# LoRA activations of a gated FFN: the 128x128 transpose moves from TensorE to DVE blocks and two DRAM transfers, and the LoRA steps are issued apart

## The chip, the cores and the metric

The kernel runs on one core of a Trainium2 chip. Time is device time in microseconds; the median of three runs counts. Profiles come from one profiled execution, whose own time is given beside its span. PE is the matrix engine (TensorE), PEld its weight loads, DVE the vector engine, ACT the scalar engine, POOL the GpSimd engine, SP the engine that only issues transfers. L with a number is a line of the kernel.

## The reference

64 batches of 64 channels and 1024 features (4096 rows in all, called tokens) first have their channels mixed by one of 16 matrices, then pass a linear layer with a mixture of eight low-rank (LoRA) experts, of which a gate takes the best two. All is float32.

```python
def _L0_cond_ref(x, weights, condition):
    W = weights[condition]                        # (64, 64, 64)
    return jnp.einsum('bct,bcd->bdt', x, W)

def _L0_ffn_ref(x, gate_w, base_w, base_b, lora_A, lora_B):
    gate_logits = jnp.einsum('bsd,ed->bse', x, gate_w)          # e = 8
    weights, selected = jax.lax.top_k(gate_logits, K)           # K = 2
    weights = jax.nn.softmax(weights.astype(jnp.float32), axis=2)
    result = jnp.einsum('bsd,od->bso', x, base_w) + base_b
    w_full = jnp.sum(jax.nn.one_hot(selected, E) * weights[..., None], axis=2)
    low = jnp.einsum('bsd,erd->ebsr', x, lora_A)                # r = 16
    lora_out = jnp.einsum('ebsr,eor,bse->bso', low, lora_B, w_full)
    return result + SCALING * lora_out

x = x + _L0_ffn_ref(_L0_cond_ref(x, ...), ...)
```

## The kernel before

**Tiles.** The 4096 tokens are 32 tiles of 128. For each tile the kernel multiplies the transposed input (`xT`) with one wide matrix of 1160 columns: 128 of LoRA A (8 experts of rank 16), 8 of the gate, 1024 of the base. The columns are cut into chunks c = 0, 1, 2 of 384, 388 and 388; chunk 0 holds LoRA A, the gate and 248 base columns. This product is called z. Mixing the channels is a product from the left, so it is done on z afterwards, with a block-diagonal 128x128 matrix (`bd`, loaded by index by `load_cond`).

**Three matmuls for one.** float32 products are made of a high and a low part (`xh`, `xl`; `wh`, `wl`; `zh`, `zl`; `bdh`, `bdl`; `lth`, `ltl`; `lbh`, `lbl`): hi x hi, hi x lo, lo x hi. ACT makes the high part (`copy`, L232), DVE the low part (`sub`, L229).

**Stages of z.** The first four tiles are plain (`PLAIN`). The other 28 go in pairs, each pair's z by 20 block products p1 to p20 of sums of blocks instead of 24 (a fast matrix product). `Operands` loads blocks of x into 18 units of `xr` and makes their sums on DVE (L290), `split_x` splits them, `zstep` (L409) issues the matmuls, `keep`, `pass_on` (L710) and `mix` (L727) recombine the results from the PSUM banks z0 to z3. The order of products is the list `ORDER`: `HEAD`, then for each further pair a mix of the last five products of one pair (`TAIL`) and those of the next; for the last two pairs the list `FINAL` (t: the earlier pair, p: the later).

**After z.** `chunk` calls `post` for each tile i and chunk c:
- c = 0: `sums` (L441) mixes the channels into bank a0 or a1. `gate` copies the 136 columns of Low and logits to `low` (L472), finds the top two and their softmax weights (L478 to L484), and scales Low by them (L485). `tr` transposes the scaled Low (128 tokens x 128) on PE against the identity into the same bank (L492), and splits it into `lth` (ACT) and `ltl` (DVE). A second `sums` adds the LoRA part, `lth`/`ltl` times `lbh`/`lbl`, onto the 248 base columns.
- c = 1, 2: one step of six matmuls, LoRA and channel sums together, into bank o0 or o1; for the last two tiles two steps, LoRA first.
- `finish` (L451) adds the bank to `xtok`, where x plus bias lies (`load_tok`: SP loads x, POOL accumulates the bias, L376); `store` sends it out, by POOL (L458), for the last two tiles by SP (L461). There are three `xtok` buffers. The first four tiles have x and bias added by POOL afterwards (`late_sum`).

**Order.** Nothing is scheduled by hand beyond `ORDER`. Each step is told to the class `Program` with an engine, a cost, what it reads and writes and a due time (`pr.horizon`); `run` then lays the steps out in planned time, and issues on each engine in that order. A step with `first` goes ahead of others 1.2 us (`MARGIN`) after its inputs are ready by the plan; a transfer is planned at 2.0 us (`FLIGHT`) plus its bytes, and the order of the products on PE is kept by the name "order". On the chip each engine works through its instructions in the planned order, and waits where an input is late; SP and POOL wait likewise before they issue a transfer.

Of the kernel before, what the change touches and what calls it, by code (L numbers as in the profile page):

```python
# [24 lines left out]
ER = E * R  # L25
SCALING = 2.0
LOWEST = -3.0e38
NTOK = B * C
NT = NTOK // P
# [3 lines left out]
N0 = NG + T - 2 * W  # L33
# [3 lines left out]
NPAIR = NT // 2  # L37
NPLAIN = 2
TOP = 3.0e38
NWARM = 39  # L40

PE, ACT, DVE, POOL, SP = "PE", "ACT", "DVE", "POOL", "SP"
# [4 lines left out]
ISSUE = 0.45  # L47
# [4 lines left out]
AHEAD = 10.0  # L52
MARGIN = 1.2
COL, SET = 0.000418, 0.014
LEAST = 0.111
PAIR = 27.3
LAG, LAST = 16.0, 8.0
SOONER = 2.0
# [4 lines left out]
            p12="f9", p13="f13", p14="r", p15="f15", p16="a11", p17="a22", p18="f18", p19="f19", p20="f11")  # L63
BANK = dict(p6="R", p16="X", p7="Q", p5="X", p19="Y", p17="X", p11="R", p13="R", p18="X", p4="Q", p20="Q", p3="X",
            p1="R", p10="X", p12="X", p14="Y", p15="Y", p2="Y", p8="Y", p9="Y")
FIRST_ONLY = ("p4", "p10", "p12", "p20")
OPENS = ("p6", "p16", "p7", "p19")
HEAD = ("p6", "p16", "p7", "p5", "p19", "p17", "p11", "p13", "p18", "p4", "p20", "p3", "p1", "p10", "p12")
TAIL = ("p14", "p15", "p2", "p8", "p9")

FINAL = "t14 p6 t15 p16 p7 t2 p5 t8 p17 t9 p11 p4 p13 p19 p18 p20 p14 p3 p10 p15 p12 p1 p2 p8 p9".split()

SPLITS = (("f6", "a11"), ("s", "f5"), ("f19", "a22"), ("f11", "f13"), ("f18", "a24"), ("f3", "f1"), ("a13", "f9"),
          ("r", "f15"), ("f2", "f8"))
# [3 lines left out]
class Program:  # L78
# [7 lines left out]
    def add(self, engine, cost, fn, reads=(), writes=(), due=None, first=False, size=0.0, early=None, port=False,  # L86
            after=0.0):

        n = len(self.steps)
        engine, cost = (e if isinstance(e, (list, tuple)) else [e] for e in (engine, cost))
        deps = set()
        for b in list(reads) + list(writes):
            if b in self.writer:
                deps.add(self.writer[b])
        for b in writes:
            deps.update(self.readers.get(b, ()))
        for b in reads:
# [67 lines left out]
def cond_ffn_kernel(ctx, tc, xT, x, idx, cw, wall, bias, lb, out):  # L167
# [21 lines left out]
    nc = tc.nc  # L189
    eng = {ACT: nc.scalar, DVE: nc.vector, POOL: nc.gpsimd}  # L190
    sb = ctx.enter_context(tc.tile_pool(name="sb", bufs=1))
    ps = ctx.enter_context(tc.tile_pool(name="ps", bufs=1, space=bass.MemoryType.PSUM))

    def many(n, shape, dt, name):
        return [sb.tile(shape, dt, name=f"{name}{j}") for j in range(n)]
# [3 lines left out]
    ident = sb.tile([P, P], F32, name="ident")  # L199
# [7 lines left out]
    lth, ltl = many(2, [P, P], F32R, "lth"), many(2, [P, P], F32R, "ltl")  # L207
    ltr = ltl[1].bitcast(F32)
    scratch = {nm: many(2, [P, w], F32, nm) for nm, w in (
        ("mx", 8), ("l2", 14), ("e", E), ("wf", E), ("s", 1), ("nm", 1), ("r", 1))}  # L210
# [14 lines left out]
    pr = Program()  # L225
    add = pr.add

    def sub(e, o, a, b):
        eng[e].tensor_tensor(o, a, b.bitcast(F32), ALU.subtract)  # L229

    def copy(e, o, a):
        (nc.scalar.copy if e == ACT else nc.vector.tensor_copy)(o, a)  # L232
# [3 lines left out]
    def take(kind, n):  # L236
        turns[kind] = turns.get(kind, -1) + 1
        return turns[kind] % n
# [67 lines left out]
    raw, hi, lo = {}, {}, {}  # L306
# [92 lines left out]
    def mm_cost(n):  # L399
        return max(COL * n + SET, LEAST)  # L400

# [62 lines left out]
    def gate(i, b):  # L464

        v = {k: t[i % 2] for k, t in scratch.items()}
        t = low[i % 2]
        lg, lg14 = t[:, ER:NG], t[:, ER:]  # L470
        zc = [("low", i % 2)]
        add(ACT, 0.3, lambda e: copy(e, t[:, :NG], bank[b][:, :NG]), [b], zc)  # L472

        def op(o, a, f, eng=DVE, cost=0.17, port=False):
            add(eng, cost, lambda e: f(), [(b, i % 2) for b in a], [(b, i % 2) for b in o], port=port)

        stt = nc.vector.scalar_tensor_tensor
# [4 lines left out]
        op(["wf", "s"], ["l2", "e"], lambda: stt(v["wf"], v["l2"][:, :E], LOWEST, v["e"], ALU.is_equal, ALU.mult,  # L482
                                                 accum_out=v["s"]), cost=0.3, port=True)
        op(["r"], ["s"], lambda: nc.vector.reciprocal(v["r"], v["s"]))  # L484
        op(["low"], ["wf", "r"], lambda: stt(  # L485
            t[:, :ER].rearrange("p (e r) -> p e r", e=E), t[:, :ER].rearrange("p (e r) -> p e r", e=E), v["r"],
            v["wf"].unsqueeze(2).broadcast_to([P, E, R]), ALU.mult, ALU.mult), cost=0.3, port=True)

    def tr(i, b):

        h, l, tp = lth[i % 2], ltl[i % 2], bank[b][:, N0:N0 + P]
        add(PE, 0.107, lambda e: nc.tensor.matmul(tp, low[i % 2][:, :ER], ident, is_transpose=True, start=False,  # L492
                                                  stop=False, skip_group_check=True),
            [("low", i % 2), "ident"], [b], first=i < NT - 2)
        add(ACT, 0.25, lambda e: copy(e, h, tp), [b], [("lth", i % 2)])
        add(DVE, 0.25, lambda e: sub(e, l, tp, h), [b, ("lth", i % 2)], [("ltl", i % 2)])

    held = {}

    def post(i, c, q):  # L500

        if c == 0:
            b = held[i] = f"a{i % 2}"
            if i >= NT - 2:
                pr.horizon -= SOONER
# [4 lines left out]
            finish(i, c, b)  # L510
            if i >= NT - 2:
                pr.horizon += SOONER
            return
        else:
            b = f"o{take('o', 2)}"
            if i >= NT - 2:
                sums(i, c, b, with_lora=True, start=True)
                sums(i, c, b, q, (0, 1, 2), stop=True)
            else:
                sums(i, c, b, q, (0, 1, 2), True, True, True)  # L520
        finish(i, c, b)


# [6 lines left out]
    t = 4.9  # L530
# [4 lines left out]
        ends_plain = t  # L535
    ORDER = [(NPLAIN, p) for p in HEAD]
    for q in range(NPLAIN, NPAIR):
        if q == NPAIR - 2:
            ORDER += [(q + (p[0] == "p"), "p" + p[1:]) for p in FINAL]
            break  # L540
        nxt = HEAD
        mixed = ("p14", nxt[0:1], "p15", nxt[1:2], "p2", nxt[2:3], "p8", "p9", nxt[3:])
        for p in mixed:
            ORDER += [(q, p)] if isinstance(p, str) else [(q + 1, n) for n in p]
    ends = {}
    for q, p in ORDER:
        for f in range(2):
# [252 lines left out]
    for q, p in ORDER:  # L800
        pr.horizon = ends[q] + (LAST if q == NPAIR - 1 else LAG)
        if q not in pairs:
            pairs[q] = Pair(q)
        if (q, p) == (NPLAIN, HEAD[3]):
            load_pair(q)
        pairs[q].product(p)
        if p == TAIL[-1] and q < NPAIR - 1:

            load_pair(q + 1)
    pr.run()  # L810
# [39 lines left out]
```

## Time and profile before

| what | us |
|---|---|
| median of three runs | 460.18 (459.96 to 460.42) |
| the profiled execution | 460.46 |
| its span, first to last instruction | 458.7 |
| PE busy | 452.3 |
| DVE busy | 383.4 |
| DVE busy in 136 to 163 us, about one pair's turn | 22.84 of 27.00 |
| ACT busy in the same stretch | 13.05 |
| chain of waits: share of PE | 93% |

The mean granted clock of PE is 1.000. A stage's PE time is read from where its matmuls start, since each takes some 340 ns and the next starts about 178 ns later. The DMA line of the page gives the mean busy share of 16 DMA engines; "us to landing" is the time from a transfer's issue until its data are there.

### The profile page before, as it was taken

The numbers are of one execution on the slowest core, as the hardware profiler recorded it, in microseconds if no ns is written. First come the engines' busy times: TensorE is split into PE (matmuls) and PEld (weight loads), VectorE is DVE, ScalarE is ACT, GpSimd is POOL, SyncE is SP. The second block draws the span as 40 slices with busy tenths as digits, with TensorE's granted clock in tenths as the row PEclk, the third lists the DMA queues.
The fourth block names the chain that finished last, engine by engine and source line by source line (L and its number), as shares of the span: only waits on it lengthen the run. The fifth ranks groups of instructions, "written<-read, shape, count | busy, mean of one in ns | idle before, by whom it ended". The sixth has DMA issues, their size and how long they took to land.

```text
span 458.7 us, 7562 instructions
## 1 busy us (share of the span) xinstructions
PE 452.3 (99%) x2615; PEld 449.0 (98%) x2615; DVE 383.4 (84%) x940; ACT 227.5 (50%) x520; POOL 88.8 (19%) x107
## 2 busy tenths in 40 slices
PE   8999999999999999999999999999999999999995
PEld 8999999999999999999999999999999999999995
DVE  5999997878989788796997979789797988888674
ACT  5864656543636345373543646355354544546231
POOL 3010215121303021120303003030120403103000
PEclk9999999999999999999999999999999999999999
DMA  8942739976778462764846566573655746456142
GB/s 284 336 126 42 160 98 205 214 215 198 176 211 202 172 161 88 215 128 167 188 137 189 119 185 150 172 181 110 196 120 177 182 128 195 114 176 148 48 137 91
DMA packets 36085, 75.00 MB, mean 164 GB/s; under 512 B 4416, under 2 KB 22096, under 8 KB 36048
## 3 DMA queue, kind: packets, MB, share of 16 engines
q0 software_dynamic: 10560, 36.72, 33.7%
q1 hardware_dynamic: 25200, 37.41, 26.0%
q10 hardware_dynamic: 288, 0.40, 0.3%
q8 instruction: 20, 0.33, 0.3%
q14 instruction: 17, 0.14, 0.1%
HBM read 57.74 MB, written 16.78 MB: 162 GB/s over the span
## 4 chain that ended last, share of the span: by engine, by line
PE 93%; DMA 5%; DVE 1%; SPq 1%; ACT 0%; issue 0%; ACTq 0%
PE ps_z L409 71%; PE ps_o L441 15%; PE ps_a L441 6%; DMA xtok<-in_lb 2%; DMA w_b<-in_w 2%; DMA xr<-in_xT 1%; PE ps_a L492 1%; SPq L324 0%; SPq L274 0%; DVE xtok L451 0%; DVE wl_b_b L229 0%; ACT wh_b_b L232 0%; DVE st L727 0%; ACTq L232 0%
## 5 line engine op out<-in xcount | busy, mean ns | idle before, releaser
L229 DVE TENSOR_TENSOR xl<-xr,xh 128x512 fp32r<-128x512 f32 (+1 forms) x138 | 92.3, 672 | 20.6 <-ACT xh L232 20.3
L409 PE MATMUL ps_z<-wh_t_p,xh 128*128 128x388 f32 (+1 forms) x308 | 105.3, 342 | 0.1
L409 PE MATMUL ps_z<-wl_t_p,xh 128*128 128x388 f32 (+1 forms) x308 | 104.3, 339 | 0.0
L409 PE MATMUL ps_z<-wh_t_p,xl 128*128 128x388 f32 (+1 forms) x308 | 104.3, 339 | 0.0
L232 ACT CAST xh<-xr 128x512 fp32r<-128x512 f32 (+1 forms) x136 | 82.5, 610 | 37.4 <-PE ps_z L409 32.8
L727 DVE TENSOR_TENSOR st<-ps_z,st 128x388 f32<-128x388 f32 x126 | 70.3, 559 | 21.0 <-PE ps_z L409 19.9
L290 DVE TENSOR_TENSOR xr<-xr 128x256 f32<-128x256 f32 (+1 forms) x139 | 69.7, 528 | 3.1 <-DMA xr<-in_xT 2.7
L409 PE MATMUL ps_z<-wh_b_p,xh 128*128 128x388 f32 (+1 forms) x180 | 61.4, 341 | 0.0
L409 PE MATMUL ps_z<-wh_b_p,xl 128*128 128x388 f32 (+1 forms) x180 | 60.8, 338 | 0.0
L409 PE MATMUL ps_z<-wl_b_p,xh 128*128 128x388 f32 (+1 forms) x180 | 60.8, 338 | 0.0
L409 PEld LDWEIGHTS ps_z<-wh_t_p,xh 128*128 128x128 f32 x308 | 57.8, 188 | 1.2 <-DVE st L727 0.7
L409 PEld LDWEIGHTS ps_z<-wl_t_p,xh 128*128 128x128 f32 x308 | 57.9, 188 | 0.0
L409 PEld LDWEIGHTS ps_z<-wh_t_p,xl 128*128 128x128 f32 x308 | 57.8, 188 | 0.0
L458 POOL DMA_DIRECT2D out<-xtok x30 | 16.8, 560 | 193.5 <-DVE xtok L451 92.2
L232 ACT CAST zh<-st 128x388 fp32r<-128x388 f32 (+1 forms) x70 | 36.2, 517 | 24.2 <-DVE st L727 17.0
L376 POOL DMA_DIRECT2D xtok<-in_bias x28 | 27.4, 980 | 97.3 <-DMA xtok<-in_x 90.0
L389 POOL DMA_INDIRECT bdr<-in_cw,rows x32 | 36.1, 1129 | 28.0 <-DVE zl L229 16.6
L710 ACT ACTIVATE ps_z<-ps_z 128x388 f32<-128x388 f32 x42 | 20.1, 478 | 41.1 <-PE ps_z L409 39.0
L451 DVE TENSOR_TENSOR xtok<-ps_o,xtok 128x388 f32<-128x388 f32 x56 | 31.0, 559 | 11.0 <-PE ps_o L441 10.6
L229 DVE TENSOR_TENSOR zl<-st,zh 128x388 fp32r<-128x388 f32 (+1 forms) x70 | 38.9, 556 | 1.5 <-ACT zh L232 1.2
L409 PEld LDWEIGHTS ps_z<-wh_b_p,xh 128*128 128x128 f32 x180 | 33.8, 188 | 0.2
L409 PEld LDWEIGHTS ps_z<-wl_b_p,xh 128*128 128x128 f32 x180 | 33.8, 188 | 0.0
(130 smaller groups left out, 871.1 us busy)
## 6 DMA issues: line engine op xcount, KB each, us to landing
xr<-in_xT SPq DMA_DIRECT2D x128, 128.0 KB, 3.1
xtok<-in_bias POOLq DMA_DIRECT2D x32, 512.0 KB, 7.2
out<-xtok POOLq DMA_DIRECT2D x30, 512.0 KB, 3.1
xtok<-in_x SPq DMA_DIRECT2D x28, 512.0 KB, 3.7
w_b<-in_w SPq DMA_DIRECT2D x10, 388.0 KB, 5.8
xtok<-in_x POOLq DMA_DIRECT2D x4, 512.0 KB, 6.2
out<-xtok SPq DMA_DIRECT2D x4, 194.0 KB, 2.5
bdr<-in_cw,rows POOLq DMA_INDIRECT x32, 5.3
```

What stands on the lines that cost most here:

```text
L229: eng[e].tensor_tensor(o, a, b.bitcast(F32), ALU.subtract)
L232: (nc.scalar.copy if e == ACT else nc.vector.tensor_copy)(o, a)
L290: add(DVE, tt_cost(2 * P * len(os)), lambda e: nc.vector.tensor_tensor(some(xr, os), some(xr, xs), some(xr, ys), f), [("xr", u) for u in s ...
L376: add(POOL, 1.1, lambda e: nc.gpsimd.dma_start(xtok[j], bias.broadcast_to([P, T]), accum_op=ALU.add), writes=keys, size=TWICE * 4.0 * T * P)
L389: add(POOL, 1.04, lambda e: nc.gpsimd.indirect_dma_start(out=bdr[j], out_offset=None, in_=cw, in_offset=bass.IndirectOffsetOnAxis(ap=rows[ ...
L409: nc.tensor.matmul(z, l[:, j, n], w.ap()[:, f, :cols], start=(start and q == 0), stop=(stop and q == 2), skip_group_check=True)
L441: nc.tensor.matmul(d, l, r, start=(start and m == 0), stop=(stop and m == len(mms) - 1), skip_group_check=True)
L451: add(DVE, 0.09 + 0.00104 * (s.stop - s.start), lambda e: nc.vector.tensor_tensor(xtok[j][:, o], bank[b][:, s], xtok[j][:, o], ALU.add), [ ...
L458: add(POOL, 1.0, lambda e: nc.gpsimd.dma_start(out[i * P:(i + 1) * P, o], xtok[j][:, o]), src, size=4.0 * P * (o.stop - o.start))
L492: add(PE, 0.107, lambda e: nc.tensor.matmul(tp, low[i % 2][:, :ER], ident, is_transpose=True, start=False, stop=False, skip_group_check=True),
L710: add(ACT, 0.2 + 0.00085 * W, lambda e: nc.scalar.mul(z[b], z[x], scale), [BANKS[x]], [BANKS[b]])
L727: add(DVE, 0.09 + 0.00104 * W, lambda e: nc.vector.tensor_tensor(unit(u), a(), b(), f), reads, [ukey(u)])
```

## The change

- For tiles 0 to 27, `tr` no longer uses PE. DVE transposes the scaled `low` within blocks of 32x32 into a new SBUF tile `ltt`. SP writes that to a DRAM tile `there`, and SP reads it back, 128 bytes at a time, so that the blocks come to their transposed places. `lth` and `ltl` are then split from `ltt` in SBUF instead of from PSUM. The rows come out in another order than before; LoRA B (`lb`) is permuted on the host to match.
- Tiles 28 to 31 (`NPE = 4`) keep the transpose on PE; their scaling writes to `ltt` in the permuted order.
- For tiles 0 to 29, the LoRA step of chunks 1 and 2 is a step of its own, after the channel sums, and the banks a0, o0, a1, o1 are taken in turn by all chunks. For tiles 30 and 31 the two banks of each kind are kept, LoRA first as before.
- The order of products is given by a list `MIX` for the middle pairs, in which p17 and p11 have changed places; `FINAL` is another order.
- `wf` is merged into `e`, and `rows` takes the place of `idx_sb` in memory.

```diff
+NPE = 4
+BLK = 32
-TAIL = ("p14", "p15", "p2", "p8", "p9")
-FINAL = "t14 p6 t15 p16 p7 t2 p5 t8 p17 t9 p11 p4 p13 p19 p18 p20 p14 p3 p10 p15 p12 p1 p2 p8 p9".split()
+MIX = "t14 p6 t15 p16 t2 p7 t8 t9 p5 p19 p11 p17 p13 p18 p4 p20 p3 p1 p10 p12".split()
+FINAL = "p6 t14 p16 p5 p7 t15 p11 t2 t8 t9 p13 p17 p19 p4 p18 p3 p10 p20 p14 p12 p15 p2 p1 p8 p9".split()
...
+    there = [dram.tile([P, P], F32, name=f"there{j}") for j in range(2)]
...
-        op(["wf", "s"], ["l2", "e"], lambda: stt(v["wf"], v["l2"][:, :E], LOWEST, v["e"], ...
+        op(["e", "s"], ["l2"], lambda: stt(v["e"], v["l2"][:, :E], LOWEST, v["e"], ...
+        if i < NT - NPE:
+            o = lambda: stt(
+                t[:, :ER].rearrange("p (e r) -> p e r", e=E), t[:, :ER].rearrange("p (e r) -> p e r", e=E), v["r"],
+                v["e"].unsqueeze(2).broadcast_to([P, E, R]), ALU.mult, ALU.mult)
+        else:
+            o = lambda: stt(
+                ltt[i % 2].rearrange("p (x r y) -> p y x r", x=2, r=R),
+                t[:, :ER].rearrange("p (y x r) -> p y x r", x=2, r=R), v["r"],
+                v["e"].rearrange("p (y x) -> p y x", x=2).unsqueeze(3).broadcast_to([P, E // 2, 2, R]),
+                ALU.mult, ALU.mult)
...
     def tr(i, b):
-        add(PE, 0.107, lambda e: nc.tensor.matmul(tp, low[i % 2][:, :ER], ident, is_transpose=True, start=False,
-                                                  stop=False, skip_group_check=True),
-            [("low", i % 2), "ident"], [b], first=i < NT - 2)
+        if i >= NT - NPE:
+            add(PE, 0.107, lambda e: nc.tensor.matmul(tp, ltt[i % 2], ident, is_transpose=True, ...
+        else:
+            raw, src, port, d = ltt[i % 2], ("ltt", i % 2), True, there[i % 2]
+            tp = raw
+            add(DVE, 0.3, lambda e: nc.vector.transpose(raw, t), [("low", i % 2)], [src])
+            add(SP, ISSUE, lambda e: nc.sync.dma_start(d, raw), [src], [("there", i % 2)],
+                size=4.0 * P * P)
+            add(SP, ISSUE, lambda e: nc.sync.dma_start(
+                tp.rearrange("p (i b) -> p i b", b=BLK),
+                d.rearrange("(i a) (j b) -> (a j) i b", a=BLK, b=BLK)), [("there", i % 2)], [src], size=8.0 * P * P)
...
     def post(i, c, q):
+        if i < NT - 2:
+            b = ("a0", "o0", "a1", "o1")[take("o", 4)]
+        else:
+            b = f"o{take('last', 2)}" if c else f"a{i % 2}"
...
-            b = f"o{take('o', 2)}"
-            if i >= NT - 2:
-                sums(i, c, b, with_lora=True, start=True)
-                sums(i, c, b, q, (0, 1, 2), stop=True)
-            else:
-                sums(i, c, b, q, (0, 1, 2), True, True, True)
+            sums(i, c, b, q, (0, 1, 2), start=True)
+            sums(i, c, b, with_lora=True, stop=True)
...
-        mixed = ("p14", nxt[0:1], "p15", nxt[1:2], "p2", nxt[2:3], "p8", "p9", nxt[3:])
+        mixed = FINAL if q == NPAIR - 2 else MIX if q < NPAIR - 2 else ()
...
-    rows = sb.tile([P, NT], U32, name="rows")
+    rows = idx_sb.bitcast(U32)
...
-        "lb": f(np.asarray(L0_ffn_lora_B).transpose(0, 2, 1).reshape(ER, T)),
+        "lb": f(np.asarray(L0_ffn_lora_B).transpose(0, 2, 1).reshape(ER // BLK, BLK, T).swapaxes(0, 1).reshape(ER, T)),
```

More of the change, by code (lines that the diff above doesn't have):

```diff
@@ L191, in cond_ffn_kernel @@
     sb = ctx.enter_context(tc.tile_pool(name="sb", bufs=1))
+    dram = ctx.enter_context(tc.tile_pool(name="dram", bufs=1, space=bass.MemoryType.DRAM))
     ps = ctx.enter_context(tc.tile_pool(name="ps", bufs=1, space=bass.MemoryType.PSUM))
@@ L206, in cond_ffn_kernel @@
     low = many(2, [P, NG + 6], F32, "low")
-    lth, ltl = many(2, [P, P], F32R, "lth"), many(2, [P, P], F32R, "ltl")
+    lth, ltl, ltt = many(2, [P, P], F32R, "lth"), many(2, [P, P], F32R, "ltl"), many(2, [P, P], F32, "ltt")
     ltr = ltl[1].bitcast(F32)
+    there = [dram.tile([P, P], F32, name=f"there{j}") for j in range(2)]
     scratch = {nm: many(2, [P, w], F32, nm) for nm, w in (
-        ("mx", 8), ("l2", 14), ("e", E), ("wf", E), ("s", 1), ("nm", 1), ("r", 1))}
+        ("mx", 8), ("l2", 14), ("e", E), ("s", 1), ("nm", 1), ("r", 1))}
     bank = {nm: ps.tile([P, 512], F32, name=f"ps_{nm}")
@@ L481, in gate @@
         op(["l2"], ["mx", "low"], lambda: nc.vector.match_replace(v["l2"], v["mx"], lg14, LOWEST), cost=0.25)
-        op(["wf", "s"], ["l2", "e"], lambda: stt(v["wf"], v["l2"][:, :E], LOWEST, v["e"], ALU.is_equal, ALU.mult,
+        op(["e", "s"], ["l2"], lambda: stt(v["e"], v["l2"][:, :E], LOWEST, v["e"], ALU.is_equal, ALU.mult,
                                                  accum_out=v["s"]), cost=0.3, port=True)
         op(["r"], ["s"], lambda: nc.vector.reciprocal(v["r"], v["s"]))
-        op(["low"], ["wf", "r"], lambda: stt(
-            t[:, :ER].rearrange("p (e r) -> p e r", e=E), t[:, :ER].rearrange("p (e r) -> p e r", e=E), v["r"],
-            v["wf"].unsqueeze(2).broadcast_to([P, E, R]), ALU.mult, ALU.mult), cost=0.3, port=True)
@@ L489, in tr @@
-    def tr(i, b):
-        h, l, tp = lth[i % 2], ltl[i % 2], bank[b][:, N0:N0 + P]
-        add(PE, 0.107, lambda e: nc.tensor.matmul(tp, low[i % 2][:, :ER], ident, is_transpose=True, start=False,
-                                                  stop=False, skip_group_check=True),
-            [("low", i % 2), "ident"], [b], first=i < NT - 2)
-        add(ACT, 0.25, lambda e: copy(e, h, tp), [b], [("lth", i % 2)])
-        add(DVE, 0.25, lambda e: sub(e, l, tp, h), [b, ("lth", i % 2)], [("ltl", i % 2)])
@@ L498, in cond_ffn_kernel @@
-    held = {}
-    def post(i, c, q):
+        if i < NT - NPE:
[8 more added lines that the diff above has]
+                ALU.mult, ALU.mult)
@@ new lines, in gate @@
+        op(["low" if i < NT - NPE else "ltt"], ["e", "r", "low"], o, cost=0.3, port=True)
+    def tr(i, b):
+        h, l, t = lth[i % 2], ltl[i % 2], low[i % 2][:, :ER]
+        tp, src, port = bank[b][:, N0:N0 + P], b, False
+        if i >= NT - NPE:
+            add(PE, 0.107, lambda e: nc.tensor.matmul(tp, ltt[i % 2], ident, is_transpose=True, start=False,
+                                                      stop=False, skip_group_check=True),
+                [("ltt", i % 2), "ident"], [b], first=i < NT - 2)
+        else:
[7 more added lines that the diff above has]
+                d.rearrange("(i a) (j b) -> (a j) i b", a=BLK, b=BLK)), [("there", i % 2)], [src], size=8.0 * P * P)
+        add(ACT, 0.25, lambda e: copy(e, h, tp), [src], [("lth", i % 2)])
+        add(DVE, 0.25, lambda e: sub(e, l, tp, h), [src, ("lth", i % 2)], [("ltl", i % 2)], port=port)
@@ L502, in post @@
+    def post(i, c, q):
+        if i < NT - 2:
+            b = ("a0", "o0", "a1", "o1")[take("o", 4)]
+        else:
+            b = f"o{take('last', 2)}" if c else f"a{i % 2}"
+        early = SOONER if i >= NT - 2 and c == 0 else 0.0
+        pr.horizon -= early
         if c == 0:
-            b = held[i] = f"a{i % 2}"
-            if i >= NT - 2:
-                pr.horizon -= SOONER
             sums(i, 0, b, q, (0, 1, 2), start=True)
@@ L509, in post @@
             sums(i, 0, b, with_lora=True, stop=True)
[L510 to L513, printed above, removed]
-        else:
-            b = f"o{take('o', 2)}"
-            if i >= NT - 2:
-                sums(i, c, b, with_lora=True, start=True)
-                sums(i, c, b, q, (0, 1, 2), stop=True)
-            else:
-                sums(i, c, b, q, (0, 1, 2), True, True, True)
+        elif i >= NT - 2:
+            sums(i, c, b, with_lora=True, start=True)
+            sums(i, c, b, q, (0, 1, 2), stop=True)
+        else:
+            sums(i, c, b, q, (0, 1, 2), start=True)
+            sums(i, c, b, with_lora=True, stop=True)
+        pr.horizon += early
         finish(i, c, b)
@@ L537, in cond_ffn_kernel @@
     for q in range(NPLAIN, NPAIR):
[L538 to L541, printed above, removed]
-        mixed = ("p14", nxt[0:1], "p15", nxt[1:2], "p2", nxt[2:3], "p8", "p9", nxt[3:])
-        for p in mixed:
-            ORDER += [(q, p)] if isinstance(p, str) else [(q + 1, n) for n in p]
+        mixed = FINAL if q == NPAIR - 2 else MIX if q < NPAIR - 2 else ()
+        ORDER += [(q + (p[0] == "p"), "p" + p[1:]) for p in mixed]
     ends = {}
@@ L806, in cond_ffn_kernel @@
         pairs[q].product(p)
-        if p == TAIL[-1] and q < NPAIR - 1:
+        if p == "p9" and q < NPAIR - 1:
             load_pair(q + 1)
```

## The prediction

> **What bounds the kernel now.** I read the page's busy shares first, then PE's waits, then the PE timeline around one transpose, then SP's waits and the DMA queues.
>
> ```profile
> PE 452.3 (99%) x2615; PEld 449.0 (98%) x2615; DVE 383.4 (84%) x940; ACT 227.5 (50%) x520; POOL 88.8 (19%) x107
> ...
> PE ps_o L223 <- DVE warm L309: 1.1, 1, 1.1
> PE ps_z L409 <- DVE wl_b_b L229: 0.2, 1, 0.2
> ...
> L492 PE MATMUL ps_a<-ident,low x32: 270/272/273, 33.9 to 449.8; 128*128 128x128 f32 x32
> ...
> 146.74 0.34 PE L409 MATMUL ps_z<-wl_t_p,xh 128*128 128x388 f32 x1
> 146.91 0.34 PE L409 MATMUL ps_z<-wh_t_p,xl 128*128 128x388 f32 x1
> 147.09 0.27 PE L492 MATMUL ps_a<-ident,low 128*128 128x128 f32 x1
> 147.11 0.42 PE L409 MATMUL ps_z<-wh_t_p,xh 128*128 128x388 f32 x1
> 147.37 0.34 PE L409 MATMUL ps_z<-wl_t_p,xh 128*128 128x388 f32 x1
> ...
> SPq L274 <- DVE xl L229: 190.4, 38, 12.9
> SPq L375 <- DMA out<-xtok: 127.5, 15, 32.0
> ...
> q1 hardware_dynamic: 25200, 37.41, 26.0%
> ...
> xr<-in_xT SPq DMA_DIRECT2D x128, 128.0 KB, 3.1
> xtok<-in_bias POOLq DMA_DIRECT2D x32, 512.0 KB, 7.2
> xtok<-in_x SPq DMA_DIRECT2D x28, 512.0 KB, 3.7
> out<-xtok SPq DMA_DIRECT2D x2, 124.0 KB, 1.9
> ```
>
> PE waits 1.3 us in the whole span by the list of waits: it issues matmuls back to back, and the time is their sum plus the head and the tail. A PE instruction taken out is worth its spacing, not its 272 ns: 388-column matmuls start 0.178 us apart (146.74, 146.91). From 146.91 to 147.37, with the transpose between, are 0.46 us for what would be two spacings, 0.355. So a transpose costs **0.11 us**. SP is the reverse: it spends over 300 us in waits for free buffers. Instructions are cheap there, but SP works in order, so waits behind waits are not.
>
> **The change, part by part.**
>
> *Transposes off PE.* The last four tiles keep theirs (NPE = 4), so 28 go: 28 x 0.11 = **-3.1 us**, all on the path. The number of other matmuls is the same: LoRA steps and channel sums of chunks 1 and 2 are only issued apart.
>
> *DVE.* 28 block transposes of 128x128. No row shows one. Nearest are L229 on 128x128 (284 ns) and the scaling L485 (348 ns); from below 0.16 us (the 8-column L482), from above twice L485, 0.7. I take 0.3. Two per pair of tiles add 0.6 us to about 23 of 27 us that DVE is busy in each such stretch: beside other work. At 0.7 they add 1.4, still inside the 4 us left. `wf` merged into `e`, and `rows` laid over `idx_sb`, cost nothing: same instructions.
>
> *The round trip.* Write 64 KB (128 packets of 512 B), then read it back as 512 pieces of 128 B. The write: 1.9 us (the 124 KB `out`) to 3.1 (`xr`); I take 2.0. The read: 32 pieces fall to each of 16 engines. Queue q1 gives a packet's mean price: 26% of 16 x 458.7 us over 25200 is 76 ns, for 1.5 KB. At 76 ns each, 32 take 2.4 us; scaled by bytes, 0.2. On the 1.9 us that even the small transfer needs, the read is 2.1 to 4.3; I take **3.4**, nearer the per-packet end. The Trainium skill speaks against this part. "VectorE: DVE Perf Modes", section "The three transpose paths", gives 128x128 to TensorE or the crossbar, and calls a plain copy that transposes by strides 19 times slower. q1 moves 37.41 MB in 26% of 458.7 us, 314 GB/s: 64 KB need 0.21 us, 19 times that is 4.0, and with the 1.9 the read is 5.9 us (an estimate). I stay with the rows, because here the pieces are runs of 128 B and DVE has done the turn inside the block; 5.9 goes to the rival.
>
> *Is the trip covered?* In the trace, the second tile of a pair has its scaled Low a median of 5.0 us after its chunk-0 sums, the first 2.3 to 5.4. Add transpose 0.3, issue 0.45, write 2.0, issue 0.45, read 3.4, hi and lo split 0.3 + 0.3, and about 0.5 of hops: **12.7 us**. Against it stands PE work: counting matmuls in the changed PE order at 0.178 us (0.11 for 248 columns), between a tile's chunk-0 sums and its first LoRA matmul lie 13.8 us at tile 0, 13.8 and 14.7 at the first tiles of pairs (6,7) and (10,11), and 15 to 24 elsewhere. In pairs (12,13), (14,15) and (18,19) SP issues the read of the first tile only behind the write of the second, whose sums come 6.2 us later: 6.2 + 5.0 + 0.3 + 0.9 of issues + 3.4 + 1.0 = 16.8 against 17.9. So five tiles (tile 0; one of (6,7), with another issue of 0.45 ahead; these three) have 0.6 to 1.1 us to spare, the others 2 to 9. For misses at these five I put **+0.5**.
>
> *SP and POOL.* 56 more issues at 0.45 us are 25 us of SP, which has over 300 idle. Queued behind SP's waits are the `xr` loads, for which DVE's sums, the splits and then PE wait. A held load has 18 `xr` units before it; DVE waited for `xr` only 2.7 us in the trace, so I put 0 there. Uncovered, each of the 28 trips could hold SP for its write's 2 us. `xtok` is tighter: the next tile's load waits for the store of an earlier one. Around tile 13, PE work from the last LoRA step of tile 10 to the end of its own first is 13 us, while finish 0.6, store 3.1, load 3.7, bias 7.2 and hops come to 15.5. Then DVE waits some 2 us at `finish`, with splits and mixes behind it. Its bank comes round again only 8 us later, so PE is not held directly; DVE's 4 idle us per pair take the wait.
>
> *Banks in turn.* Four PSUM banks instead of two and two fixed ones. The shortest way from a bank's last LoRA step to its next sums is 2.1 us in the PE order; the finishing add is 0.41 to 0.56. Zero; were DVE 1.5 us behind, each reuse of that kind (ten of them) would cost what is missing.
>
> *Order of products.* In MIX only p17 and p11 change places: p11 now follows p5 after one product (1.06 us), and needs `pass_on` into its bank, 0.48 us plus hops: 0. In FINAL, p5 follows p16 in the same bank with three matmuls (0.53 us) between, while ACT must first copy the bank out (0.48 + hops 0.25): **+0.3**. At the very end both tiles' transposes stand directly ahead of the LoRA matmuls. In the trace the first of them starts at 446.18, its hi copy ends at 446.82 and its lo part at 447.16, with twelve matmuls in between as cover. Without these, PE waits: **+0.6**. The short stalls before (0.4 at 439.8, 0.3 at 446.2) I leave as they are.
>
> *Start.* The load of the last weight block now goes out ahead of the slot that waited for `lb` (landed 21.04 us, load out at 21.51, PE short of 0.4 us around 26.7): between 0 and -0.4, I take **-0.2**.
>
> Sum: -3.1 + 0.5 + 0.3 + 0.6 - 0.2 = **-1.9 us**. The profiled execution took 460.46 us (span 458.7), so 458.6; the median of the runs is 460.18, 0.3 below, so **458.3 us**. This kernel's measurement can tell about 0.2% (0.9 us) from no change.
>
> **Rivals.**
>
> *The read-back is dear (slower).* Its place is SP's second transfer, ahead of `lth` and of PE's LoRA step. With x us over my 3.4 the tiles lose what exceeds their cover. At x = 1.4, a read of 4.8 us, the five tight tiles lose about 2 us and the gain is all but gone: the point from which it decides. At the skill's 5.9 (x = 2.5) they lose about 1.5 + 1.9 + 3 x 1.4, and a sixth 0.5: 8.1 us in place of 0.5, +5.7 net, **465.9 us**. For it: 7.2 us for `bias` and a worst landing of 11.1 us for `xr` show what contention does, and SP can be held behind an `xtok` load. Against it: the core's DMA engines are about 60% busy, and in the steady part `xr` lands in 2.6 us. Chance 0.22.
>
> *DVE falls behind at finish (slower).* The `xtok` turn is late by more than DVE's slack, and `xl` and `zl` come late for PE. A wait of 2.5 us plus 0.6 of transposes in 12 pairs against 4 us of slack costs nothing on average, but it comes in one lump: at 0.5 us of PE per pair, +6 - 1.9, **464.3 us**. For it: DVE is the second fullest engine. Against it: PE never waited for DVE in steady work. Chance 0.12.
>
> *The gain is eaten.* The tail at 1.5 and the tight tiles at 1.5 us instead of my 0.9 and 0.5: -0.3, **459.9 us**. Chance 0.09.
>
> That the change does not do what it says is excluded for PE: the changed order holds exactly 28 matmuls fewer.
>
> **How the numbers follow.** My forecast gets 0.57: 456.8 (everything covered, the start gains its 0.4: -3.5) to 459.2. So faster 0.57, same 0.09, slower 0.34. The range goes from 456.8 up to 466.0, which takes in both slower cases' own times; what remains above is a read-back beyond 6 us.
>
> **What would show it.** PE without waits at `lth` and `ltl` except at the end; 28 fewer `ident` matmuls; the read-back's landing at 3 to 4 us; the block transpose near 0.3 us. Wrong, if the list of waits names PE or its weight loads at the LoRA line for more than 2 us, if DVE waits at `finish` and PE at `xl` behind it, or if the read-back takes over 4.8 us.

## The result, and the profile after

The changed kernel takes **482.3 us** (median of four runs, 478.57 to 489.44) beside 460.12 us for the kernel before on the same chip: 22 us slower where 1.9 us less was forecast. Ratios here and below, this one 1.045 [1.040, 1.051], are of the means of fast runs, that is without those over 1.5% above the fastest of their kernel (here 489.44). The changed kernel's runs spread over 11 us, those of the kernel before over half a microsecond. The profiled execution took 478.57 us, its span is 476.8 us.

The page first: busy time, the queues, the chain that ended last, and the transfers with their median time to landing.

```profile
PE 458.2 (96%) x2587; PEld 451.1 (95%) x2587; DVE 386.4 (81%) x968; ACT 227.5 (48%) x520; POOL 88.6 (19%) x107
...
q0 software_dynamic: 10560, 36.72, 31.9%
...
PE 73%; DMA 16%; DVE 6%; issue 2%; ACT 1%; SPq 1%; POOL 0%; DVEq 0%; POOLq 0%
...
xr<-in_xT SPq DMA_DIRECT2D x128, 128.0 KB, 5.7
...
there<-ltt SPq DMA_DIRECT2D x28, 64.0 KB, 2.9
ltt<-there SPq DMA_DIRECT2D x28, 64.0 KB, 4.4
```

PE has its 28 matmuls less (2615 to 2587) and is yet busy 5.9 us longer: its mean granted clock is 0.989 instead of 1.000, which on 476.8 us is some 5 us (an estimate). DMA now holds 16% of the chain, which was 5%. The new transfers land at the median in 2.9 and 4.4 us for the priced 2.0 and 3.4, and a row that was not touched has moved: the `xr` loads land in 5.7 us instead of 3.1. The next list is that of waits, PE's and then DVE's and SP's; its columns are the total, the number and the longest.

```profile
PE ps_a L446 <- ACT lth L237: 4.6, 3, 2.4
PE ps_z L414 <- DVE st L745: 2.8, 3, 1.5
PE ps_z L414 <- ACT xh L237: 2.6, 1, 2.6
PE ps_a L446 <- DVE ltl L234: 1.8, 1, 1.8
...
DVE xr L295 <- DMA xr<-in_xT: 18.8, 14, 3.9
...
SPq L516 <- DVE ltt L515: 99.1, 13, 14.7
SPq L380 <- DMA out<-xtok: 64.4, 12, 19.5
...
SPq L518 <- DMA there<-ltt: 32.7, 17, 5.2
```

PE waits at the LoRA line, as the forecast said it would if it was wrong. DVE waits 18.8 us for `xr`, which was 2.7. And SP, which had waited almost only for free buffers, now stands before the write until DVE has transposed (99.1 us), and before the read until the write has landed (32.7).

**One stall, followed back.** At 217 us PE loses 1.8 us. The timelines of PE and DVE, with start, duration and, in brackets, the idle time before and its releaser:

```profile
217.00 0.33 PE L414 MATMUL ps_z<-wh_t_p,xl 128*128 128x384 f32 x1
218.98 0.38 PE L446 MATMUL ps_a<-lbh,lth 128*128 128x248 f32 x1 [1.65 <-ACT lth L237]
...
220.64 0.52 PE L414 MATMUL ps_z<-wh_t_p,xh 128*128 128x384 f32 x1
```

```profile
218.96 0.29 DVE L234 TENSOR_TENSOR ltl<-ltt,lth 128x128 fp32r<-128x128 f32 x1 [4.17 <-ACT lth L237]
219.17 0.56 DVE L745 TENSOR_TENSOR st<-ps_z,st 128x388 f32<-128x388 f32 x1
```

DVE stands 4.17 us at `ltl`, with `st` and `xl` for other products queued behind. The stall costs PE a second time: from 220.64 on its matmuls start 0.32 us apart instead of 0.17 to 0.18. In the profile the granted clock is at half from 220.5 us for 3.4 us; the row of this stretch (busy time and, in brackets, instructions of PE, PEld, DVE, ACT and POOL, then PE's clock, DMA share, GB/s) has a mean clock of 0.83:

```profile
220.00:230.00 10.00, 10.00 (x50) 10.00 (x49) 8.02 (x18) 3.31 (x7) 0.72 (x2) 0.83 0.35 85
```

Why the read was late is in SP's timeline of that stretch (of consecutive issues of one kind the first start and the time until the last are given):

```profile
205.47 0.33 SPq L516 DMA_DIRECT2D there<-ltt  x1
205.90 4.98 SPq L380 DMA_DIRECT2D xtok<-in_x  x2
210.98 0.37 SPq L516 DMA_DIRECT2D there<-ltt  x1
211.40 0.42 SPq L518 DMA_DIRECT2D ltt<-there  x1
211.92 3.33 SPq L279 DMA_DIRECT2D xr<-in_xT  x5
215.34 0.58 SPq L518 DMA_DIRECT2D ltt<-there  x1
```

The first tile's write landed after 1.5 us, at 207.0. Its read goes out only at 211.40: the second `xtok` load, ahead of it, needs a buffer whose store lands at 210.5. So at 211 everything that SP held goes out at once, a second write, two reads and the `xr` loads, and in the same moments POOL issues two bias accumulates:

```profile
210.99 0.95 POOL L381 DMA_DIRECT2D xtok<-in_bias  x1 [4.89 <-DMA xtok<-in_x]
214.70 0.88 POOL L381 DMA_DIRECT2D xtok<-in_bias  x1 [2.76 <-DMA xtok<-in_x]
```

The two reads take 7.2 and 7.9 us to land. From 205.47 to 218.60 the first trip took 13.1 us; the forecast had 6.3 from write to landing. In the kernel before, two accumulates go out just as close (220.86 and 224.56), but little that is urgent stands beside them: SP had issued seven `xr` loads 12 us ahead of the `xtok` loads, and they landed in 2.3 to 2.6 us. Its timeline there:

```profile
204.92 5.27 SPq L274 DMA_DIRECT2D xr<-in_xT  x7
217.34 0.33 SPq L375 DMA_DIRECT2D xtok<-in_x  x1
218.53 0.33 SPq L274 DMA_DIRECT2D xr<-in_xT  x1
218.96 0.37 SPq L375 DMA_DIRECT2D xtok<-in_x  x1
```

Nearly alone, the trip is cheaper than forecast: those of tiles 0 and 1, at 32 to 40 us, where the DMA engines are 0.16 to 0.21 busy, write in 1.5 us and read in 2.1. Later the write takes 1.5 to 7.7 us and the read 2.0 to 8.6.

**The start.** The rebuilt plan also put a copy of `bdh` early in ACT's order. Its data come at 12.5 us, and ACT stands 3.84 us for them (the first line of ACT's timeline below), with the splits behind it that PE needs: the wait of 2.6 us at `xh` in the list.

```profile
12.53 0.30 ACT L237 CAST bdh<-bdr 128x128 fp32r<-128x128 f32 x1 [3.84 <-DMA bdr<-in_cw,idx_sb]
```

Summing for every PE matmul its start spacing beyond the normal one (0.178, 0.174 and 0.111 us for 388, 384 and 248 columns) tells where PE loses time. "Slow" is spacing near 0.32 us; "LoRA" and "z" name the matmul that came late; "end" is the last 32 us. These sums are worked out from the PE timelines.

| us lost by PE | first 30 us | slow | at LoRA | at z | end |
|---|---|---|---|---|---|
| before | 1.4 | 0.6 | 0.5 | 1.5 | 0.9 |
| after | 5.8 | 4.7 | 7.2 | 4.9 | 1.8 |

### The profile page after: what moved, and what is told of

The parts are those of the page before. It is cut to its first block, busy times and chain, and to the rows that moved or that the text cites. A ratio compares the mean times of both kernels' runs of the same rounds, so it can differ in the third digit from the quotient of the medians.

```text
span 476.8 us, 7687 instructions
## 1 busy us (share of the span) xinstructions
PE 458.2 (96%) x2587; PEld 451.1 (95%) x2587; DVE 386.4 (81%) x968; ACT 227.5 (48%) x520; POOL 88.6 (19%) x107
## 3 DMA queue, kind: packets, MB, share of 16 engines
q0 software_dynamic: 10560, 36.72, 31.9%
## 4 chain that ended last, share of the span: by engine, by line
PE 73%; DMA 16%; DVE 6%; issue 2%; ACT 1%; SPq 1%; POOL 0%; DVEq 0%; POOLq 0%
PE ps_z L414 56%; PE ps_o L446 9%; PE ps_a L446 8%; DMA xr<-in_xT 5%; DMA ltt<-there 4%; DMA out<-xtok 2%; DVE xl L234 2%; DMA xtok<-in_bias 2%; DVE st L745 1%; DMA xtok<-in_x 1%; DMA bdr<-in_cw,idx_sb 1%; DVE xr L295 1%; DMA idx_sb<-in_idx 1%; DVE xtok L456 1%; DVE zl L234 0%
## 5 line engine op out<-in xcount | busy, mean ns | idle before, releaser
L295 DVE TENSOR_TENSOR xr<-xr 128x256 f32<-128x256 f32 (+1 forms) x139 | 71.3, 526 | 19.0 <-DMA xr<-in_xT 18.8
L381 POOL DMA_DIRECT2D xtok<-in_bias x28 | 25.7, 919 | 121.6 <-DMA xtok<-in_x 121.4
L394 POOL DMA_INDIRECT bdr<-in_cw,idx_sb x32 | 36.7, 1147 | 53.8 <-DVE bdl L234 27.4
L414 PEld LDWEIGHTS ps_z<-wh_b_p,xl 128*128 128x128 f32 x180 | 34.2, 190 | 0.0
```

The source lines that it names most:

```text
L295: add(DVE, tt_cost(2 * P * len(os)), lambda e: nc.vector.tensor_tensor(some(xr, os), some(xr, xs), some(xr, ys), f), [("xr", u) for u in s ...
L381: add(POOL, 1.1, lambda e: nc.gpsimd.dma_start(xtok[j], bias.broadcast_to([P, T]), accum_op=ALU.add), writes=keys, size=TWICE * 4.0 * T * P)
L394: add(POOL, 1.04, lambda e: nc.gpsimd.indirect_dma_start(out=bdr[j], out_offset=None, in_=cw, in_offset=bass.IndirectOffsetOnAxis(ap=rows[ ...
L414: nc.tensor.matmul(z, l[:, j, n], w.ap()[:, f, :cols], start=(start and q == 0), stop=(stop and q == 2), skip_group_check=True)
```

## The experiments

Times are medians, ratios those to the kernel before on the same chip (459.9 to 460.3 us). The first theory was that the trip's transfers, in company, are too slow for their cover; the rivals were the new orders, the start, and LoRA issued apart.

A change to a step's engine, cost or time makes `run` lay out everything anew. Where that happens, as in 4, 6, 7 and 14 to 16, PE's order agrees with the changed kernel's in only a third to two thirds of its instructions, so the change is not isolated. The traces show the same order on PE, DVE, ACT and SP in the changed kernel and runs 5, 8 and 11, in the kernel before and run 9, in runs 6 and 10, and in runs 12 and 13. These comparisons are the clean ones.

**1. No trips.** All transposes on PE, everything else as changed.

```diff
-NPE = 4
+NPE = NT
```

> NPE = 32: every tile keeps its transpose on TensorE; the LoRA steps apart, the banks in turn and both new orders of products stay. If the round trip through DRAM is the whole loss: 459 to 461.5 us, PE waits under 2 us. If the banks or the orders cost a part: above 464 us, with PE waiting at the sums or at p11 and p5.

Measured: 462.2 us, 1.005 [1.004, 1.007], between the two ranges. So 20 of the 22 us come with the trips and the plan that they bring, and 2 from the rest.

**2. The orders alone.** The kernel before with `MIX` and the new `FINAL`.

> The kernel before with the two new orders of products alone. If the orders are harmless: 459.5 to 461 us. If they cost: 463 us or more, with waits of PE at the products that changed places.

Measured: 463.1 us, 1.007 [1.006, 1.009]: +3.2 us. In the first experiment's PE timeline the step where `FINAL` lets p5 follow p16 reads so:

```profile
417.67 0.34 PE L414 MATMUL ps_z<-wh_t_p,xl 128*128 128x388 f32 x1
418.58 0.45 PE L414 MATMUL ps_z<-wh_d_p,xh 128*128 128x388 f32 x1 [0.57 <-ACT st L237]
```

0.91 us for a spacing of 0.18: 0.73 lost, where 0.3 was forecast. Four more gaps were not forecast: 0.73 and 0.81 near 438 us in `FINAL`, and 0.42 and 0.34 at 108 and 138 us in `MIX`. The last two are not in the first experiment, which has the same `MIX`: parts of the change do not simply add.

**3. LoRA apart and banks in turn alone.** The first experiment with the old orders.

```diff
+NPE = NT
-FINAL = "p6 t14 p16 ..."          # and MIX: the old lists and loop
+FINAL = "t14 p6 t15 ..."
```

> Transposes on TensorE for all tiles and the old order of products; of the change only the LoRA steps apart and the banks in turn are left (and the permuted rows of Low). The two orders alone cost 3.2 us, and with all three but the trips the loss was 2.3. If the parts add: 0.9 us faster than before, 458.5 to 459.7 us. If the parting is worth nothing with the old order: 460 us.

Measured: 460.9 us, 1.0019 [1.0011, 1.0027]: +0.9 us, no gain. With the orders' 3.2 that would be 4.1, while all three together (run 1) cost 2.3.

**4. A plan that knows the trip is slow.** `run` lays out with 1.5 us more for the write and 3.5 for the read.

```diff
-                size=4.0 * P * P)
+                size=4.0 * P * P, extra=1.5)
...
-   [("there", i % 2)], [src], size=8.0 * P * P)
+   [("there", i % 2)], [src], size=8.0 * P * P, extra=3.5)
```

> The changed kernel; only the plan reckons the write 1.5 us and the read 3.5 us longer, so that PE work between a tile's sums and its first LoRA matmul grows from 14 to 22 us to 17 to 25 us. Theory A, the trip is late only because the plan took it too short: PE no longer waits at lth and ltl, 457 to 460 us. Theory B, SP's waits in order hold back the loads of xr as well: waits at lth go, those at xh, xl and st stay, 465 to 475 us. Theory C, the transfers themselves load the DMA engines: no better than 476 us.

Measured: 484.7 us, 1.053 [1.049, 1.057]. Of the three theories only C allowed that. PE's loss at LoRA falls from 7.2 to 1.3 us, but that at z rises from 4.9 to 12.0, and that of the last 32 us from 1.8 to about 7. DVE's wait for `xr` halves, to 9.1 us, and the time does not fall. So with more cover planned, the loss comes out elsewhere; the plan is another one, and what LoRA's own wait costs is not shown by it.

**5. Whole rows.** The read takes rows of 512 B instead of 128 B pieces.

```diff
-                tp.rearrange("p (i b) -> p i b", b=BLK),
-                d.rearrange("(i a) (j b) -> (a j) i b", a=BLK, b=BLK)), ...
+                tp, d), ...
```

> The changed kernel, but the read takes whole rows of 512 B: the blocks stay where they are, so the LoRA part is computed from blocks in wrong places. If the 512 pieces of 128 B are what makes the read slow: it lands in 2 to 3 us in place of 4.4, and the time falls to 460 to 468 us. If it is traffic of other transfers and the queue: it still lands in 3.5 us or more at the median, 8 us at worst, and the time stays within 474 to 484 us.

Measured: 475.9 us, 1.035 [1.033, 1.037]; the read's median landing 4.0 instead of 4.4 us. The pieces are some 6 of the 22 us.

**6. The start put right.**

```diff
-   add(ACT, 0.28, lambda e: copy(e, bdh[j], bdr[j]), [("bdr", j)], [("bdh", j)])
+   add(ACT, 0.28, lambda e: copy(e, bdh[j], bdr[j]), [("bdr", j)], [("bdh", j)], after=14.0 if i < 2 else 0.0)
```

> The changed kernel; only the copies of the channel matrices of tiles 0 and 1 (bdh) are held back in the plan to 14 us, so that ACT splits the weights first. In the changed kernel ACT stood 3.8 us before that copy. If that wait is a loss of its own: the PE time lost in the first 30 us falls from 5.8 to 1.5 us, and the whole is 4 us shorter, 474 to 479 us. If the start is only cover for a later wait: no change, 479 to 486 us.

Measured: 471.3 us, 1.023 [1.020, 1.026]. That is 11 us, more than the 4.4 that PE loses at the start over before. The rest comes with another plan and is not explained.

**7. The trips on POOL.** Both transfers issued by POOL instead of SP.

> The changed kernel; only both transfers of the round trip are issued by POOL in place of SP. If SP's waits in order are what delays the xr loads: xr lands again in about 3 us at the median, DVE's wait for xr falls from 19 us to under 6, and the time is 463 to 472 us. If the traffic on the DMA engines is the cause: xr stays at 5 us, and the time at 476 us or more. If POOL's own waits take the place of SP's: waits at lth grow, 480 us or more.

Measured: 477.7 us, 1.041 [1.037, 1.046]. Only 4.6 us come back. SP has no trip to wait for any more, and yet `xr` lands in 5.1 us and DVE waits 21.7 us for it. SP's waits at the trips are thus not needed for late `xr` loads, at least in this plan, where POOL waits for the trips, with stores and accumulates behind them.

**8. No bias accumulates.** In the changed kernel the accumulates of tiles 4 to 31 are not issued.

```diff
-        add(POOL, 1.1, lambda e: nc.gpsimd.dma_start(xtok[j], bias.broadcast_to([P, T]), accum_op=ALU.add),
+        add(POOL, 1.1, lambda e: None,
```

> The changed kernel with the same plan and the same order, but the accumulating transfers of the bias of tiles 4 to 31 aren't issued, so those outputs lack the bias. If these transfers crowd the round trip: the write lands in 2 us and the read in 2.5 us at the median, PE's waits at lth and ltl go, 464 to 472 us. If the length of the trip is of SP's order and the xr and x loads alone: landings and time stay (476 us or more).

Measured: 462.0 us, 1.005 [1.003, 1.006]: 20 us come back, with everything else in the same order. SP's timeline of this kernel, the page's landings, and three lines of the lists of waits:

```profile
204.38 4.65 SPq L380 DMA_DIRECT2D xtok<-in_x  x2
209.14 0.37 SPq L516 DMA_DIRECT2D there<-ltt  x1
209.56 0.43 SPq L518 DMA_DIRECT2D ltt<-there  x1
210.08 2.92 SPq L279 DMA_DIRECT2D xr<-in_xT  x5
```

```profile
xr<-in_xT SPq DMA_DIRECT2D x128, 128.0 KB, 3.3
...
there<-ltt SPq DMA_DIRECT2D x28, 64.0 KB, 2.1
ltt<-there SPq DMA_DIRECT2D x28, 64.0 KB, 3.1
```

```profile
DVE xr L295 <- DMA xr<-in_xT: 0.8, 2, 0.4
```

```profile
SPq L516 <- DVE ltt L515: 101.2, 14, 14.6
SPq L380 <- DMA out<-xtok: 62.5, 11, 19.7
```

SP is held at the `xtok` loads as before and lets the same bundle go at 209 us. But without accumulates beside it, it lands in time, and PE waits neither at LoRA nor at z (0.0 and 0.3 us). One rival was that a missing accumulate frees the `xtok` buffers sooner and so shortens SP's waits. It falls: SP waits as long before the write (101.2 us, was 99.1) and before the `xtok` loads (62.5, was 64.4), while DVE's wait for `xr` falls from 18.8 to 0.8 us.

**9. The yardstick.** The kernel before without the same accumulates.

> The kernel before with the bias accumulates of tiles 4 to 31 not issued (their bias is missing from the output): the yardstick for the run above. Theory (PE was never held by this traffic before the change): 459.7 to 460.3 us, ratio 0.999 to 1.001. Rival (the accumulates cost the kernel before as well, and what the changed kernel gains without them is no sign of a collision with the trips): 458.5 us or less.

Measured: 460.25 us, 1.0005 [0.9997, 1.0013]. The accumulates cost the kernel before nothing that can be told from noise. So the loss needs both sides, the trips' plan and the accumulates.

**10. Without accumulates, and the start put right** (8 and 6 together).

> The changed kernel with the bias accumulates of tiles 4 to 31 not issued (their bias is missing from the output) and the bdh copies of tiles 0 and 1 held back until after the first splits. The same without the second edit took 462.0 us, with 4.4 us more lost in the first 30 us than before. Theory (the loss is the accumulates' traffic plus the start): 457.0 to 458.6 us, PE's loss in the first 30 us about 1.4 us, no wait of PE over 0.5 us at the LoRA matmuls ahead of the last 32 us. Rival (the trips cost something of their own, accumulates or not): 460 us or more.

Measured: 462.85 us, 1.006 [1.005, 1.007]: the theory's 457.0 to 458.6 fails. PE's loss in the first 30 us does fall, from 5.6 to 0.8 us; but at z and in the last 32 us together it rises from 2.0 to 6.6. The delayed copy makes another plan all the way down. So the start is a real loss, though mending it by this change gives nothing back here, and the forecast time was not reached by any version with 28 trips. Beside run 6, which has this order on PE, DVE, ACT and SP, the accumulates cost 8.5 us: how much the collision takes depends on the plan.

**11. Plain instead of accumulating.** The bias is written over `xtok`, in the same places.

```diff
-        add(POOL, 1.1, lambda e: nc.gpsimd.dma_start(xtok[j], bias.broadcast_to([P, T]), accum_op=ALU.add),
+        add(POOL, 1.1, lambda e: nc.gpsimd.dma_start(xtok[j], bias.broadcast_to([P, T])),
```

> The changed kernel with the bias of tiles 4 to 31 written over xtok instead of accumulated into it, same queue, same places (the output lacks x for these tiles). Theory (an accumulate takes more of the DMA engines than a plain transfer of as many bytes, and that is what the trips collide with): 464 to 473 us, trips' landings between those without the accumulates (2.1 and 3.1 us) and those with them (2.9 and 4.4). Rival (any 512 KB transfer there does it): 478 us or more.

Measured: 465.0 us, 1.011 [1.009, 1.012]: 17 of the 22 us come back for the same bytes on the same queue in the same order. The queue's row shows what differs (packets, MB, share of 16 engines' time):

```profile
q0 software_dynamic: 10560, 36.72, 24.6%
```

31.9% of a 476.8 us span are 152 us of all engines, 24.6% of 463.8 us are 114: accumulating, 28 transfers take 38 us more, 1.4 us each (from the 15.4% that are left without them, a plain one takes 1.5 us, an accumulating one 2.9). In the stall's stretch the engines were full. The 9 us from the first of two accumulates on, in the changed kernel, in the kernel before, and in this run (columns as above):

```profile
211.00:220.00 9.00, 7.35 (x42) 7.00 (x41) 4.83 (x11) 2.78 (x7) 1.81 (x2) 1.00 0.96 222
```

```profile
221.00:230.00 9.00, 9.00 (x53) 8.96 (x52) 8.24 (x29) 5.46 (x15) 3.97 (x4) 1.00 0.94 181
```

```profile
210.70:219.70 9.00, 8.89 (x52) 8.55 (x51) 6.10 (x14) 3.37 (x8) 1.08 (x2) 1.00 0.94 291
```

With accumulates the engines are 0.96 busy at 222 GB/s, without accumulating 0.94 busy at 291. They are as full in the kernel before (0.94), and PE loses nothing there: what matters is that the changed kernel has loads and trips in this stretch that PE soon needs.

**12 and 13. Trips that nothing needs.** Next came the question whether the trips' bytes or SP's waits do the harm. Both runs add 28 trips, whose data nobody uses, to the kernel before. In the first, SP waits neither for Low nor for the write that it has just issued; in the second it does.

```diff
+            d, src = there[i % 3], there[(i - 1) % 3 if i else 0]
+            add(SP, ISSUE, lambda e: nc.sync.dma_start(d, ident), [("low", i % 2)], [("there", i % 2)],
...
# second run:
+            d = src = there[i % 3]
+            add(SP, ISSUE, lambda e: nc.sync.dma_start(d, low[i % 2][:, :ER]), [("low", i % 2)], [("there", i % 2)],
...
```

> The kernel before, all transposes on TensorE and the old orders, plus 28 trips that nothing computes with: SP writes 64 KB from a constant to DRAM and reads 64 KB in 128 B pieces of an earlier such write, placed in SP's order where the changed kernel's trips stand, but with no wait for Low and none of the read for its own write. Only the traffic of the trips is added. Theory (their traffic delays the xr loads and DVE with them): xr's median landing rises from 3.1 to over 4.5 us, DVE's wait for xr from 2.7 to over 8 us, 463 to 475 us. Rival (SP's waits at the trips hold the xr loads back, bytes are harmless): xr stays at 3.1 to 3.6 us, 459.8 to 461 us.

> The same as the run above, but the write takes the scaled Low, and so waits for DVE, and the read takes what was just written, and so waits for the landing: SP is held as in the changed kernel, while PE waits for none of it. Theory (traffic): within 2 us of the run above. Rival (SP's waits): 465 us or more, at least 4 us above the run above. Third way (the loss needs LoRA to wait for the trip itself): both runs under 461 us.

Measured: 461.96 us, 1.0036 [1.0023, 1.0049], and 465.8 us, 1.011 [1.009, 1.014]. DVE's wait for `xr` in the lists of waits, first without SP's waits, then with them:

```profile
DVE xr L293 <- DMA xr<-in_xT: 4.4, 4, 2.2
```

```profile
DVE xr L293 <- DMA xr<-in_xT: 10.0, 6, 3.0
```

`xr` lands in 2.9 us in the first and 3.8 in the second. The bytes cost 1.7 us, together with the plan that they bring; SP's waits cost 3.9 more (PE, DVE, ACT and POOL have the same instructions in the same order in both). The traffic theory, which wanted both runs alike, falls; the rival's 465 is met, its distance of 4 us just missed, and the first run's time lies between their ranges. In the profiled second run one stall makes up about all of the difference: at 97.9 and 102.9 us accumulates go out beside a trip's read and `xr` loads, DVE waits 2.98 us for `xr` until 106.7, PE loses 3.2 us at 108, and its granted clock is at half for 3.4 us from 111.9. It is the same collision again.

**14. The `xr` loads off SP.** In the changed kernel ACT issues them from the third pair on.

```diff
+        on, q = (SP, nc.sync) if i < 4 else (ACT, nc.scalar)
-        add(SP, ISSUE, lambda e: nc.sync.dma_start(
+        add(on, ISSUE, lambda e: q.dma_start(
...
-            size=8.0 * P * P)
+            size=8.0 * P * P, early=True)
```

> The changed kernel with the xr loads of all pairs from the third on (i from 4 on) issued by ACT, on a queue and an order of their own, so that SP's waits at the trips and at xtok no longer stand in front of them; trips and accumulates stay. Theory (SP's order drives the xr loads onto the accumulates; that is the larger part of the loss): xr's median landing back under 4.2 us, DVE's wait for xr under 8 us, 465 to 474 us. Rival (the traffic of trips and accumulates delays the loads wherever they are issued, as pool_trip hinted with 5.1 us and 21.7 us): over 5 us and 15 us, 476 us or more.

Measured: 471.9 us, 1.028 [1.024, 1.032]; DVE's wait for `xr` falls to 8.5 us, just over the theory's 8. But the loads still land in 5.3 us. Neither side has it whole: with the loads off SP the kernel is 10 us shorter, and beside trips and accumulates they land late wherever they are issued. The 10 us are not the price of SP's order, since the plan is another; run 6 gains 11 with the loads on SP.

**15. Half the trips**, those of each pair's first tile, with old orders and the start put right:

> The old orders of products, the bdh copies held back, and the round trip through DRAM only for the first tile of each pair (14 trips); the second tile's transpose stays on TensorE. LoRA steps apart and banks in turn as in the changed kernel. Theory (each trip that meets the accumulates and the queue on SP costs PE some 0.5 us on average, and two trips in a row hold each other up): 14 transposes less are worth 1.5 us, LoRA apart and banks in turn cost 0.9, what the trips lose in contention is at most half of the changed kernel's 11 or so: 460 to 466 us. Rival (the loss is the second trip of a pair waiting behind the first): 458.8 to 460.2 us, faster than the kernel with only LoRA apart and banks in turn (460.9).

Measured: 461.9 us, 1.004 [1.003, 1.006]. Inside the theory's 460 to 466; some 1 us slower than no trips at all (460.9, on another chip).

**16. All trips, old orders, start put right.**

> The changed kernel with 28 trips, the old orders of products and the bdh copies held back: only the trips, the LoRA steps apart and the banks in turn remain. Theory (start, orders and collision add up): 482.3 less 11 for the start and about 3 for the orders, 465 to 470 us; PE still waits for lth or ltl in several places of over 1 us. Rival (the new orders were what gave the trips their cover, so that the old ones have less): over 471 us. Rival (the collision needed the disturbed start): under 461 us.

Measured: 485.3 us, 1.050 [1.046, 1.054]. The sum of parts fails by 15 us: it is over 471, as the rival of less cover had it. Less cover itself is not shown: the plan is another, and which of the old orders' steps does it was not tried.

## Why the prediction was wrong

**The step that failed** is this: "DVE waited for `xr` only 2.7 us in the trace, so I put 0 there". It took the landings of the old trace for those of the changed kernel. With "25 us of SP, which has over 300 idle" it also took the idle time of a queue for room, though it had said itself that "waits behind waits" are not cheap. SP's idle time is waiting, in order, and a trip adds two waits that stand in front of the `xr` loads; these then go out beside the accumulates. The wait that got 0 measured 18.8 us.

What the clean comparisons show: without the accumulates, in the same order and with waits of SP as long before the writes and the `xtok` loads, that wait is 0.8 us and 20 of the 22 us are gone (17 where they are plain); the kernel before does not feel the accumulates; and SP's waits cost 3.9 us where LoRA does not depend on the trip. So the cause is one collision, of the trips and the loads issued with them on one side and the accumulates on the other. How its loss divides between late `xr` loads and the trip's own late landing stays open: the wait for `xr` alone does not set the time, which was 484.7 us with 9.1 us of it (run 4) and 477.7 with 21.7 (run 7).

**The read, 3.4 us** ("nearer the per-packet end"), and **the write, 2.0**: both too dear nearly alone (2.1 and 1.5), both too cheap in work (medians 4.4 and 2.9, up to 8.6 and 7.7; eleven of the 28 reads took over the 4.8 us of the forecast's sign). The bounds were built from what the transfer is; what is beside it decides. The rival "the read-back is dear" named the right place and the right evidence, the 7.2 us of `bias`. Its price of 5.9 us, from the section "The three transpose paths" in "VectorE: DVE Perf Modes" of the Trainium skill, has the wrong reason: nearly alone the read needs 2.1 us, and with whole rows the median is still 4.0. The section's 19 compares with a transpose by the crossbar and is stated for a large innermost stride of the destination; the forecast put it on the time of plain loads. The loss was nearly four times the rival's 5.7. That "the core's DMA engines are about 60% busy" was a mean, over stretches of 0.94 already in the kernel before.

**Tight tiles, +0.5.** PE lost 7.2 us at LoRA. The cover of 13.8 to 24 us was compared with a trip of uncontended durations, 6.3 us from write to landing where the one followed above took 13.1. SP issuing the first read behind the second write was forecast for three pairs; in six pairs it stood behind the second `xtok` load, and went out some 4 us (3.6 to 4.6) after the write had landed.

**Clock.** Left out. The granted clock is at half for 3.4 us from 15.7, 220.5 and 251.2 us, after PE lost 2.8, 1.8 and 2.5 us at 11, 217 and 248 us; about ten matmuls each time then start 0.32 us apart ("slow" in the table, 4.7 us with 0.6 before). Losses of 2.0 and 1.6 us at 365 and 371 us were not followed by it. The Trainium skill's "TensorE: Matmul & The Clock Gate" (section "HAM oscillation — how this bites in real kernels") asks that PE not idle for more than some 3.4 us; here less sufficed three times, though not each time.

**Start, -0.2.** It became +4.4 in PE's loss (5.8 against 1.4). Of the moved steps one weight load was looked at; the copy of `bdh`, which the new plan puts ahead of splits of `xh`, was not.

**Orders.** +0.3 for `FINAL`, 0 for `MIX`: alone +3.2 together. The step p16 to p5 was right in kind and measured 0.73; gaps of 0.73 and 0.81 near it were not forecast. The transposes ahead of LoRA at the end, +0.6, lost 0.5 at 466 us. **Banks in turn and LoRA apart**, 0: +0.9.

**Right:** the transpose on DVE, 0.3 us (303 ns measured); 28 matmuls fewer; a wait of DVE at `finish` (5.5 us in three waits; whether PE pays for any of it is not shown). The saving of 3.1 us could not be isolated: without accumulates PE's time outside the first 30 us is 4.4 us shorter than with no trips, of which other waits are a part.

**Open:** besides the division above, how the plan's shifts make 471 or 485 us of nearly the same work (6 and 16), and how much of the loss is DVE's lateness feeding back into the next trip. No version tried beats the kernel before.

## What to carry to other kernels

A queue that mostly waits is not free: before adding a transfer that waits, list what it stands in front of, and ask when that will now go out and what it will meet. Test a suspect by taking it out without moving anything else: here changes that brought another plan moved the time by some 10 us for reasons of their own. Price a small transfer in the company it will have, not alone: look at the DMA share in the slices where it falls, not at the mean. And a matmul of 0.11 us on a full PE is a cheap price for a dependency that needs no other queue.

## What the hardware showed that was not expected

- Accumulating costs the DMA engines: 28 transfers of 512 KB take 1.4 us of all 16 engines more each than plain ones of the same bytes (31.9% of 476.8 us beside 24.6% of 463.8).
- A 64 KB write and its read-back in 128 B pieces take 1.5 and 2.1 us with the DMA engines 0.16 to 0.21 busy, and up to 7.7 and 8.6 in the changed kernel's traffic.
- Whole rows of 512 B shorten the median read only from 4.4 to 4.0 us.
- A PE stall of 1.8 us at 217 us was followed by 3.4 us at half the granted clock, with matmuls 0.32 us apart; one of 2.0 us at 365 us was not.
